# Layer 0's attention of a four-layer graph network: first masks on VectorE, cleared margins, a pool for early-freed tiles, 256-column matmuls

## The chip, the cores and the metric

The kernel runs on one core of one Trainium2 chip. A core has five engines with a queue each, worked off in order: TensorE (PE in the profile; PEld is its weight load), VectorE (DVE), ScalarE (ACT), GpSimd (POOL) and SyncE (SP, here only a queue of DMAs). They meet through semaphores. The metric is the device time of the kernel in microseconds, lower is better; the profiler's span of one execution stands beside it.

## What is computed

The reference has four layers over 16 graphs of 1024 nodes with 128 features. Each layer adds its result to x and normalises the rows.

```python
x = _layernorm(x + _L0_gnn_ref(x, adj, ...))              # attention over neighbours
x = _layernorm(x + _L1_gnn_ref(x, adj, nodemask, ...))    # dilated pattern, three convolutions
x = _layernorm(x + _L2_gnn_ref(x, adj, ...))
x = _layernorm(x + _L3_gnn_ref(x, adj, ...))

def _L0_gnn_ref(node_features, adjacency, ...):
    h_self = node_features @ W_self_w + W_self_b
    h_nb = node_features @ W_nb_w + W_nb_b
    pre = (h_self @ A1_i)[:, :, None, :] + (h_nb @ A1_j)[:, None, :, :] + A1_b
    scores = (relu(pre) @ A2_w)[..., 0] + A2_b[0]
    scores = where(adjacency == 0, -1e9, scores)
    attn = softmax(scores, axis=-1)
    return relu(h_self + einsum('bij,bjf->bif', attn, h_nb))
```

Only layer 0 is changed, and how layer 1's first stage gets its memory. The adjacency is sparse: an edge exists with a chance of about 0.8%, and it exists in both directions or in none, so the kernel handles edges and not pairs of nodes.

## The kernel before

Four phases follow each other: `phase_att` (layer 0), `phase_pattern` (the dilated pattern of layer 1), `phase_conv` (its convolutions) and `phase_end` (the rest of layer 1, and layers 2 and 3). A layer of tiles and pools records the operations, a scheduler orders each engine's instructions when the program is built, and waits are put in from what each tile's readers and writers are. Within an engine the built order is fixed.

**Blocks of attention.** The 1024 nodes of a graph are cut into NG = 10 groups of W = 104 (the last has 88). A block is a pair of groups (i, j) with i <= j; there are 55 for a graph, of which ten are diagonal (i = j, "one way": each edge is met once, in the direction in which it counts). Five bands r of 11 blocks each hold the groups r and 9 - r. A band has three chunks of 4, 4 and 3 blocks. A block has at most 128 edges, one for a partition.

**masks(b)** (L261) reads ten strips of the transposed adjacency into `ld` (two buffers), turns them into 0 and 1 in `mt` (L268), takes the diagonal out (L270), and writes the strip to `mask_d` in memory for the pattern phase (L271). All of it is on POOL and the SP queue. There are two mask tiles MT, cleared whole at the start (L162), and two tiles QS (L165).

**projections(b)** (L274): for ten groups, one fp32 matmul of the group's features with four weight matrices side by side (L287, 512 columns: h_nb, the two halves of `pre`, h_self), then one BF16 matmul of ones with the rows `bias3` (L288, 512 columns, of which the first and third quarter are zeros). ACT and DVE split the result into two fp32r parts (L291, L295).

**blocks(b, r)** (L306) finds the edges of a band: counts (L315, needs all ten masks), ranks (L345, written to `qs` by L348), slots (L327, L368), and the one-hot tiles of both ends of every edge (L376, L380).

**gather(b, r, lo, hi)** (L403) fetches, block by block, the projected rows of both ends of 128 edges: two matmuls with the one-hot tile of the own end (L423), two with that of the other end (L428), 384 columns each, into one PSUM bank `pg` of four quarters. Quarters 1 and 2 are then `pre` in the two directions, quarters 0 and 3 the neighbours' values. DVE makes the scores (L436), ACT the exponentials (L440) and the weighted values (L442). A diagonal block uses quarters 1 and 3 alone.

**scatter** (L447) sums the weighted values to the nodes (L455, fp32, two passes a matmul) into three PSUM banks; **collect** copies them out, **finish** (L477) does the softmax's division, the residual and the normalisation on POOL and DVE, and writes `x1_d` and, transposed, `x1T_d`.

The main loop weaves these generators: the gather of one chunk runs beside the scatter of the one before, the masks and projections of the next graph, the blocks of the next band, and the finish of the graph before. Ahead of it stand, for graph 0, masks and projections together, and then blocks(0, 0).

**Pools.** `phase_att` has one pool `cp` for what lives long and others that rotate. `phase_pattern` opens a pool `kp` for its constants and then `mp` with three buffers `m` of 16 KB a partition for whole masks (L743). They take the memory of the pools of attention, and a DMA into them waits for the last use of what lay there.

Of the kernel before, what the change touches and what calls it, by code (L numbers as in the profile page):

```python
# [10 lines left out]
F32 = mybir.dt.float32  # L11
F32R = mybir.dt.float32r
BF16 = mybir.dt.bfloat16
F16 = mybir.dt.float16
# [3 lines left out]
ALU = mybir.AluOpType  # L18
# [4 lines left out]
B, N, F = 16, 1024, 128  # L23
P = 128
# [68 lines left out]
NG, W, C = 10, 104, 128  # L93
# [4 lines left out]
UNITS = NG + 1  # L98
# [45 lines left out]
def phase_att(ctx, tc, t, c, x1_d, x1T_d, mask_d, flags):  # L144

    nc = tc.nc
    cp = ctx.enter_context(tc.tile_pool(name="t_c", bufs=1))
    lp = ctx.enter_context(tc.tile_pool(name="t_l", bufs=2))
    sm = ctx.enter_context(tc.tile_pool(name="t_s", bufs=4))
# [2 lines left out]
    ps_a = ctx.enter_context(tc.tile_pool(name="t_pa", bufs=1, space=PSUM))  # L152

    def load(name, shape, dtype=F16):
        w = cp.tile(shape, dtype, name=name)
        nc.sync.dma_start(w, t[name])
        return w


    MT = [cp.tile([P, NG, (NG - 1) * W + P], F16, name=f"mask{i}") for i in range(2)]  # L160
    for m in MT:
        nc.gpsimd.memset(m, 0.0)  # L162
    QS = [cp.tile([P, UNITS, C], F16, name=f"qs{i}") for i in range(2)]
    for q in QS:
        nc.gpsimd.memset(q, 0.0)  # L165
    k_rank = load("k_rank", [P, E])
    k_offs = load("k_offs", [P, P])
    k_step = load("k_step", [P, P])
    k_slot = load("k_slot", [P, C])
    k_slot_edge = load("k_slot_edge", [P, C], F32)  # L170
    k_id_col = load("k_id_col", [P, 1])
    w_all = cp.tile([P, 4 * F], F32, name="w_all")
    bias3 = cp.tile([P, 4 * F], BF16, name="bias3")
    off_diag = cp.tile([P, W], F16, name="off_diag")
    nc.vector.tensor_scalar(off_diag, c.ident[:, :W], 0.0, None, op0=ALU.is_equal)
    zeros = cp.tile([P, 512], BF16, name="zeros")
    nc.vector.memset(zeros, 0.0)
    ones = cp.tile([P, W], BF16, name="ones_w")
    nc.vector.memset(ones, 1.0)


# [1 line left out]
    k_id = load("k_id", [P, W])  # L183
    w_a2 = cp.tile([P, F], F32, name="w_a2")
    nc.sync.dma_start(w_a2, row_broadcast(t["L0_gnn_A2_w"], F))
    with tc.tile_pool(name="t_w", bufs=1) as wp:
        def weight(name, src, shape=[P, F]):
            w = wp.tile(shape, F32, name=name)
            nc.sync.dma_start(w, src)
            return w  # L190

        wsT = weight("wsT", t["wsT"])
        wnT = weight("wnT", t["wnT"])
        a1_i = weight("a1_i", t["L0_gnn_A1_w"][0:F, :])
        a1_j = weight("a1_j", t["L0_gnn_A1_w"][F : 2 * F, :])
        nc.sync.dma_start(w_all[:, :F], t["L0_gnn_W_nb_w"])
        nc.sync.dma_start(w_all[:, 3 * F :], t["L0_gnn_W_self_w"])
        pw = ps_w.tile([P, 512], F32, name="pw")
        nc.tensor.matmul(pw[:, :F], wsT, a1_i, start=True, stop=True)
        nc.tensor.matmul(pw[:, F : 2 * F], wnT, a1_j, start=True, stop=True)  # L200
        nc.scalar.copy(w_all[:, F : 3 * F], pw[:, : 2 * F])

        bs = weight("bs", t["L0_gnn_W_self_b"].rearrange("(p o) -> p o", o=1), [P, 1])
        bn = weight("bn", t["L0_gnn_W_nb_b"].rearrange("(p o) -> p o", o=1), [P, 1])
        bs_all = wp.tile([P, P], F32, name="bs_all", tag="wsT")
        nc.vector.tensor_copy(bs_all, bs.to_broadcast([P, P]))
        bn_all = wp.tile([P, P], F32, name="bn_all", tag="wnT")
        nc.vector.tensor_copy(bn_all, bn.to_broadcast([P, P]))
        a1_b = weight("a1_b", row_broadcast(t["L0_gnn_A1_b"], F))
        row_s = weight("row_s", row_broadcast(t["L0_gnn_W_self_b"], F))  # L210
        row_n = weight("row_n", row_broadcast(t["L0_gnn_W_nb_b"], F))
        pw = ps_w.tile([P, 512], F32, name="pw")
        nc.tensor.matmul(pw[:, :F], bs_all, a1_i, start=True, stop=False)
        nc.tensor.matmul(pw[:, :F], bn_all, a1_j, start=False, stop=True)
        bias = wp.tile([P, 2, F], F32, name="bias")
        nc.vector.tensor_tensor(bias[:, 0, :], pw[:, :F], a1_b, ALU.add)
        nc.vector.tensor_tensor(bias[:, 1, :], row_s, row_n, ALU.add)
        rows = wp.tile([P, 2, F], F32, name="rows")
        part = wp.tile([P, 2, F], BF16, name="part")
        for k in range(3):  # L220
            nc.vector.tensor_copy(part, bias)
            nc.vector.tensor_tensor(bias, bias, part, ALU.subtract)
            if k == 0:
                nc.vector.tensor_scalar(rows, part, c.ident[:, 0:1], None, op0=ALU.mult)
            else:
                nc.vector.scalar_tensor_tensor(
                    rows, part, c.ident[:, k : k + 1], rows, op0=ALU.mult, op1=ALU.add
                )
        nc.vector.memset(bias3, 0.0)
        nc.vector.tensor_copy(bias3.rearrange("p (a f) -> p a f", f=F)[:, 1:4:2, :], rows)  # L230

    self_edge = cp.tile([P, B, NG], F32, name="self_edge")
    nc.sync.dma_start(self_edge, t["adj_diag"])
# [27 lines left out]
    def masks(b):  # L261

        mt = MT[b % 2]
        for s in range(NG):
            n = W if s < NG - 1 else LAST
            ld = lp.tile([P, N], F32, name="ld")
            nc.sync.dma_start(ld[:n], t["adjT"][b, s * W : s * W + n, :])
            nc.gpsimd.tensor_scalar(mt[:n, s, :N], ld[:n], 0.0, None, op0=ALU.is_gt)  # L268
            d = mt[:n, s, s * W : (s + 1) * W]
            nc.gpsimd.tensor_tensor(d, d, off_diag[:n], ALU.mult)  # L270
            nc.sync.dma_start(mask_d[b, s * W : s * W + n, :], mt[:n, s, :N])  # L271
            yield

    def projections(b):  # L274

        d = S[b] = Consts()
        xT = lp.tile([P, NP], F32, name="xT", bufs=1)
        nc.sync.dma_start(xT, t["xTp"][b])
        d.parts = {}
        d.hs = lp.tile([P, NG, F], F32, name="hs")  # L280
        d.sc = lp.tile([P, BANDS * UNITS * 2], F32, name="sc")
        nc.vector.memset(d.sc, 0.0)
        d.off = lp.tile([P, BANDS * UNITS], F32, name="off")
        nc.vector.memset(d.off, 0.0)
        for s in (*range(4, NG), *range(4)):
            pw = ps_w.tile([P, 512], F32, name="pw")
            nc.tensor.matmul(pw[:W], xT[:, s * W : (s + 1) * W], w_all, start=True, stop=False)  # L287
            nc.tensor.matmul(pw[:W], ones, bias3, start=False, stop=True)  # L288
            hi = d.parts[s] = lp.tile([P, 2, 3 * F], F32R, name=f"parts{s}", bufs=1 if s < 4 else 2)
            z = sm.tile([P, F], F32, name="z_self", bufs=2)  # L290
            nc.scalar.copy(hi[:W, 0, :], pw[:W, : 3 * F])  # L291
            nc.scalar.copy(d.hs[:W, s, :], pw[:W, 3 * F :])
            nc.scalar.copy(z[:W], pw[:W, 2 * F : 3 * F])
            yield
            nc.vector.tensor_tensor(hi[:W, 1, :], pw[:W, : 3 * F], hi[:W, 0, :], ALU.subtract)  # L295

            nc.vector.tensor_tensor(z[:W], pw[:W, F : 2 * F], z[:W], ALU.add)
            k = b * NG + s
            nc.vector.scalar_tensor_tensor(
                z[:W], z[:W], 0.0, w_a2[:W], op0=ALU.max, op1=ALU.mult, accum_out=seen_self[:W, k : k + 1]  # L300
            )
            yield
# [89 lines left out]
        nc.scalar.copy(wide.ids, pw[:, : 2 * UNITS])  # L392
        yield

    def reversed_parts(x):

        return bass.AP(
            tensor=x.tensor, offset=x.offset + 2 * F, ap=[list(x.ap[0]), [-F, 3], [1, F]]
        )

    G = {}
# [1 line left out]
    def gather(b, r, lo, hi):  # L403

        d = S[b]
        wide = OH[b, r]
        todo = band(r)
        n = 2 * (hi - lo)
# [7 lines left out]
        for u in range(lo, hi):  # L416
            i, j = todo[u]
            own, other = wide.ends[:W, u, 0, :], wide.ends[:W, u, 1, :]

            pg = ps_g.tile([P, 4, F], F32, name="pg")  # L420
            flat = pg.rearrange("p a f -> p (a f)")
            for p in range(2):
                nc.tensor.matmul(  # L423
                    flat[:, : 3 * F], own, d.parts[i][:W, p, :], start=p == 0, stop=False,
                    skip_group_check=True,
                )
            for p in range(2):
                nc.tensor.matmul(  # L428
                    pg[:, 1:, :], other, reversed_parts(d.parts[j][:W, p, :]), start=False, stop=p == 1,
                    skip_group_check=True,  # L430
                )
            at = (r * UNITS + u) * 2
            ways = 2 if j > i else 1
            for e in range(ways):
                junk = sm.tile([P, F], F32, name="junk", bufs=2)
                nc.vector.scalar_tensor_tensor(  # L436
# [40 lines left out]
    def finish(b):  # L477
# [21 lines left out]
        for s0 in range(0, NG, 5):  # L499
            s = slice(s0, s0 + 5)  # L500
            shape = [W, 5, F]
            h = own[:W, s, :]
            nc.gpsimd.tensor_tensor(h, h, es[:W, s].unsqueeze(2).to_broadcast(shape), ALU.mult)
            nc.gpsimd.tensor_tensor(h, h, d.sums[:W, s, :F], ALU.add)
            yield
            nc.vector.tensor_tensor(h, h, rz[:W, s].unsqueeze(2).to_broadcast(shape), ALU.mult)
            yield
# [137 lines left out]
def phase_pattern(ctx, tc, t, c, mask_d, slots_d, x1_d, keep, flags):  # L645
# [3 lines left out]


    nc = tc.nc
    kp = ctx.enter_context(tc.tile_pool(name="q_k", bufs=1))
    mp = ctx.enter_context(tc.tile_pool(name="q_m", bufs=3))
    cp = ctx.enter_context(tc.tile_pool(name="q_c", bufs=1))
    wp = ctx.enter_context(tc.tile_pool(name="q_w", bufs=2))
    sm = ctx.enter_context(tc.tile_pool(name="q_s", bufs=4))
# [1546 lines left out]
```

## Time and profile before

| | |
|---|---|
| time, median of three | 3260.76 us (3250.69 to 3261.46) |
| span of the profiled execution | 3262.6 us, granted clock 0.921 |
| first gather matmul (L423) | 83.5 us |
| last scatter matmul ends (L455) | 1716.7 us |
| first matmul of the pattern phase (L749) | 1745.0 us |

How to read it: in the page's first section, busy time is given for each engine with its share of the span and the number of instructions. In the rows of groups stand line, engine, operation, out and in, shapes, count, busy time, mean duration in ns, and the idle time just before with what ended it. These are the rows of the lines concerned:

```profile
L268 POOL TENSOR_SCALAR mask<-ld 104x1024 f16<-104x1024 f32 (+1 forms) x160 | 464.9, 2906 | 331.6 <-PE pg L428 173.1
L423 PE MATMUL pg<-parts,oh 104*128 104x384 f32 x1760 | 560.2, 393 | 0.4 <-ACT hg L442 0.2
L428 PE MATMUL pg<-parts,oh 104*128 104x384 f32 x1760 | 498.6, 355 | 0.0
L288 PE MATMUL pw<-bias,ones_w 128*104 128x512 bf16 x160 | 63.4, 398 | 4.8 <-DVE bias L230 4.8
```

[...]the pace of PE is therefore read from starts. The granted clock is 1 at full speed and 0.5 at half.

### The profile page before, as it was taken

What the parts mean: (1) busy time and instruction counts of PE and PEld (TensorE: products, weight loads), DVE (VectorE), ACT (ScalarE), POOL (GpSimd) and SP (SyncE); (2) the same over time, 40 slices, a digit from 0 to 9 for tenths busy, and PEclk for the clock granted to TensorE, in tenths of its full rate; (3) what the DMA queues carried; (4) which work ended last, traced back from release to release, by engine and by line L of the source; (5) the groups of instructions that cost most, each with busy time, mean ns of one, the idle gap of its engine ahead of it and who ended that gap; (6) DMA issues with size and microseconds to landing.
All of it is one profiled execution on the core that took longest, in us unless ns stands there. A gap on an engine that the chain in (4) does not pass through costs nothing. (4 is left out here: it accounts for less than half of the span.)

```text
span 3262.6 us, 70599 instructions
## 1 busy us (share of the span) xinstructions
PE 2852.2 (87%) x25724; PEld 2516.6 (77%) x25724; DVE 2277.8 (70%) x8203; ACT 1785.6 (55%) x5608; POOL 1357.1 (42%) x1302
## 2 busy tenths in 40 slices
PE   3999999999999999999995859567877799999997
PEld 1878887778878887778885858356676799999997
DVE  3788788888878887888874476755655466666665
ACT  1777777777766776777771323135644343333332
POOL 7655554555545454554223332233432333322221
PEclk7999999999999999999996778788988899999999
DMA  4423332333222332322004433034443444444341
GB/s 122 121 81 84 99 89 55 84 87 105 81 60 77 97 97 60 84 81 73 21 21 166 163 105 117 27 119 149 161 158 117 156 170 170 153 168 163 141 157 37
DMA packets 162021, 348.60 MB, mean 107 GB/s; under 512 B 14708, under 2 KB 68230, under 8 KB 161536
## 3 DMA queue, kind: packets, MB, share of 16 engines
q1 hardware_dynamic: 150912, 315.57, 30.4%
q0 software_dynamic: 10752, 28.42, 3.0%
q8 instruction: 206, 3.38, 0.4%
q14 instruction: 151, 1.24, 0.1%
HBM read 257.87 MB, written 87.03 MB: 106 GB/s over the span
## 5 line engine op out<-in xcount | busy, mean ns | idle before, releaser
L268 POOL TENSOR_SCALAR mask<-ld 104x1024 f16<-104x1024 f32 (+1 forms) x160 | 464.9, 2906 | 331.6 <-PE pg L428 173.1
L423 PE MATMUL pg<-parts,oh 104*128 104x384 f32 x1760 | 560.2, 393 | 0.4 <-ACT hg L442 0.2
L455 PE MATMUL pa<-hg,we 128*104 128x129 f32 (+1 forms) x3520 | 551.4, 274 | 3.5 <-ACT hg L442 2.5
L436 DVE SCALAR_TENSOR_TENSOR junk<-pg,w_a 128x128 f32<-128x128 f32 x1600 | 402.7, 283 | 209.0 <-PE pg L428 206.3
L442 ACT ACTIVATE hg<-pg,hg 128x128 f32<-128x128 f32 x1600 | 511.7, 369 | 16.6
L455 PEld LDWEIGHTS pa<-hg,we 128*104 128x104 f32 x3520 | 494.8, 173 | 22.7 <-ACT hg L442 10.4
L428 PE MATMUL pg<-parts,oh 104*128 104x384 f32 x1760 | 498.6, 355 | 0.0
L428 PEld LDWEIGHTS pg<-parts,oh 104*128 104x128 f32 x1760 | 322.2, 192 | 1.4
L423 PEld LDWEIGHTS pg<-parts,oh 104*128 104x128 f32 x1760 | 286.8, 192 | 29.2 <-ACT hg L442 4.2
L440 ACT ACTIVATE hg<-sc 128x2 f32<-128x2 f32 (+1 forms) x880 | 186.5, 212 | 175.8 <-DVE junk L436 173.1
L410 DVE TENSOR_TENSOR we<-k_id,ids 128x832 f32<-128x832 f16 (+1 forms) x240 | 247.7, 1032 | 5.1 <-PE pa L455 3.5
L1332 POOL TENSOR_TENSOR rstd<-ve,mhalf 128x4 f32<-128x4 f32 x96 | 97.2, 1012 | 325.0 <-DVE ve L1331 324.9
L380 ACT CAST oh<-oh_b 104x1024 fp32r<-104x1024 bf16 (+1 forms) x240 | 223.2, 969 | 15.7 <-DVE oh_b L376 15.3
L287 PE MATMUL pw<-w_all,xT 128*104 128x512 f32 x320 | 178.5, 642 | 10.7 <-DMA xT<-in_xTp 8.2
L490 POOL TENSOR_TENSOR own<-parts 104x128 f32<-104x128 f32 x160 | 89.9, 597 | 222.5 <-DVE x_rows L510 211.0
L327 DVE TENSOR_TENSOR g<-k_slot,off 105x1408 f16<-105x1408 f16 x80 | 133.4, 1668 | 57.4 <-ACT off L323 57.4
L1336 DVE TENSOR_SCALAR x<-x,mv,rstd 128x128 f32<-128x128 f32 x256 | 104.7, 450 | 91.1 <-POOL rstd L1332 91.1
L376 DVE TENSOR_TENSOR oh_b<-pw,k_slot_edge 104x512 bf16<-104x512 f32 (+1 forms) x240 | 147.1, 635 | 10.1 <-PE pw L375 9.3
L355 DVE SCALAR_TENSOR_TENSOR one_way<-qs,mask 104x1040 bf16<-104x1040 f16 (+9 forms) x160 | 149.0, 931 | 1.0 <-ACT qs L348 0.9
L348 ACT CAST qs<-pw 104x416 f16<-104x416 f32 (+1 forms) x240 | 114.9, 479 | 63.1 <-PE pw L345 61.8
L369 ACT CAST oh_b<-pw 104x512 bf16<-104x512 f32 (+1 forms) x240 | 133.0, 555 | 18.3 <-PE pw L368 18.2
L1441 ACT ACTIVATE y<-x,shift,rstd 128x128 f32<-128x128 f32 x128 | 52.7, 482 | 163.4 <-POOL shift L1434 163.4
(352 smaller groups left out, 6777.9 us busy)
## 6 DMA issues: line engine op xcount, KB each, us to landing
ld<-in_adjT SPq DMA_DIRECT2D x144, 416.0 KB
m<-mask_d SPq DMA_DIRECT2D x16, 2048.0 KB
keep_adj<-in_adjT SPq DMA_DIRECT2D x8, 4096.0 KB
adj<-in_adjT SPq DMA_DIRECT2D x8, 4096.0 KB
mask_d<-mask SPq DMA_DIRECT2D x144, 208.0 KB
hT_d<-uT SPq DMA_DIRECT2D x48, 512.0 KB
h<-hT_d SPq DMA_DIRECT2D x48, 512.0 KB
hT<-hT_d SPq DMA_DIRECT2D x32, 512.0 KB
```

The source lines that it names most:

```text
L268: nc.gpsimd.tensor_scalar(mt[:n, s, :N], ld[:n], 0.0, None, op0=ALU.is_gt)
L287: nc.tensor.matmul(pw[:W], xT[:, s * W : (s + 1) * W], w_all, start=True, stop=False)
L355: nc.vector.scalar_tensor_tensor(junk[:W, :nb, :], q[:W, at : at + nb, :W], EDGE, mt[:W, i, i * W : NP].rearrange("p (n w) -> p n w", w=W) ...
L376: nc.vector.tensor_tensor(o[:W, n0 : n0 + m, 1, :], pw[:W, :m, :], k_slot_edge[:W].unsqueeze(1).to_broadcast([W, m, C]), ALU.is_equal,)
L380: nc.scalar.copy(wide.ends[:W, n0 : n0 + m], o[:W, n0 : n0 + m])
L410: nc.vector.tensor_tensor(we[:, :n, :], k_id.unsqueeze(1).to_broadcast([P, n, W]), wide.ids[:, 2 * lo : 2 * hi].unsqueeze(2).to_broadcast( ...
L423: nc.tensor.matmul(flat[:, : 3 * F], own, d.parts[i][:W, p, :], start=p == 0, stop=False, skip_group_check=True,)
L428: nc.tensor.matmul(pg[:, 1:, :], other, reversed_parts(d.parts[j][:W, p, :]), start=False, stop=p == 1, skip_group_check=True,)
L436: nc.vector.scalar_tensor_tensor(junk, pg[:, 1 + e, :], 0.0, w_a2, op0=ALU.max, op1=ALU.mult, accum_out=d.sc[:, at + e : at + e + 1],)
L440: nc.scalar.activation(hg[:, u - lo, :ways, F], d.sc[:, at : at + ways], AF.Exp)
L442: nc.scalar.activation(hg[:, u - lo, e, :F], pg[:, 3 - 3 * e, :], AF.Copy, scale=hg[:, u - lo, e, F : F + 1])
L455: nc.tensor.matmul(PA[bank][:W, at : at + part.stop - part.start], we[:, 2 * (u - lo) + e, :], hg[:, u - lo, e, part], start=False, stop=T ...
```

## The change

Six edits, all in attention or at its borders:

- **First masks on DVE.** For graph 0 the strips are loaded through ScalarE's queue and turned into masks by DVE; for the other graphs nothing changes. The purpose is that nothing at the start stands behind POOL.
- **Margins only.** Of MT and QS, only what no mask or rank ever writes is cleared.
- **A pool for early-freed tiles.** What is last used before attention's final steps lies in a pool `ep` opened first; `phase_pattern` opens `mp` ahead of `kp`, so that the mask buffers lie where `ep` was and can be filled before attention has ended.
- **Bias with 256 columns.** `bias3` holds the two quarters that aren't zero, and L288 adds into these two alone.
- **One-way blocks with 256 columns.** For a diagonal block, L423 computes quarters 1 and 2, and L428 adds to quarters 1 and 3.
- **The last finish on DVE.** For graph 15, two operations of `finish` go from POOL to DVE.

```diff
+    ep = ctx.enter_context(tc.tile_pool(name="t_e", bufs=1))
     cp = ctx.enter_context(tc.tile_pool(name="t_c", bufs=1))
...
-        w = cp.tile(shape, dtype, name=name)
+        w = (cp if name == "k_id" else ep).tile(shape, dtype, name=name)
...
-    MT = [cp.tile([P, NG, (NG - 1) * W + P], F16, name=f"mask{i}") for i in range(2)]
+    MT = [ep.tile([P, NG, (NG - 1) * W + P], F16, name=f"mask{i}") for i in range(2)]
     for m in MT:
-        nc.gpsimd.memset(m, 0.0)
-    QS = [cp.tile([P, UNITS, C], F16, name=f"qs{i}") for i in range(2)]
+        nc.gpsimd.memset(m[:W, :, N:], 0.0)
+        nc.gpsimd.memset(m[64:W, NG - 1, :N], 0.0)
+    QS = [ep.tile([P, UNITS, C], F16, name=f"qs{i}") for i in range(2)]
     for q in QS:
-        nc.gpsimd.memset(q, 0.0)
+        nc.gpsimd.memset(q[:W, :, W:], 0.0)
...
-    w_all = cp.tile([P, 4 * F], F32, name="w_all")
-    bias3 = cp.tile([P, 4 * F], BF16, name="bias3")
-    off_diag = cp.tile([P, W], F16, name="off_diag")
+    w_all = ep.tile([P, 4 * F], F32, name="w_all")
+    bias3 = ep.tile([P, 2, F], BF16, name="bias3")
+    off_diag = ep.tile([P, W], F16, name="off_diag")
...
-        nc.vector.memset(bias3, 0.0)
-        nc.vector.tensor_copy(bias3.rearrange("p (a f) -> p a f", f=F)[:, 1:4:2, :], rows)
+        nc.vector.tensor_copy(bias3, rows)
...
+        engine, queue = (nc.gpsimd, nc.sync) if b else (nc.vector, nc.scalar)
...
-            nc.sync.dma_start(ld[:n], t["adjT"][b, s * W : s * W + n, :])
-            nc.gpsimd.tensor_scalar(mt[:n, s, :N], ld[:n], 0.0, None, op0=ALU.is_gt)
+            queue.dma_start(ld[:n], t["adjT"][b, s * W : s * W + n, :])
+            engine.tensor_scalar(mt[:n, s, :N], ld[:n], 0.0, None, op0=ALU.is_gt)
...
-            nc.gpsimd.tensor_tensor(d, d, off_diag[:n], ALU.mult)
+            engine.tensor_tensor(d, d, off_diag[:n], ALU.mult)
...
-            nc.tensor.matmul(pw[:W], ones, bias3, start=False, stop=True)
+            nc.tensor.matmul(
+                pw[:W].rearrange("p (a f) -> p a f", f=F)[:, 1::2, :], ones, bias3, start=False, stop=True,
+                skip_group_check=True,
+            )
...
-            tensor=x.tensor, offset=x.offset + 2 * F, ap=[list(x.ap[0]), [-F, 3], [1, F]]
+            tensor=x.tensor, offset=x.offset + 2 * F, ap=[list(x.ap[0]), [-F * step, 4 - step], [1, F]]
...
+            ways = 2 if j > i else 1
+            first, step = (0, 1) if ways == 2 else (F, 2)
             for p in range(2):
                 nc.tensor.matmul(
-                    flat[:, : 3 * F], own, d.parts[i][:W, p, :], start=p == 0, stop=False,
+                    flat[:, first : 3 * F], own, d.parts[i][:W, p, first:], start=p == 0, stop=False,
...
-                    pg[:, 1:, :], other, reversed_parts(d.parts[j][:W, p, :]), start=False, stop=p == 1,
+                    pg[:, 1::step, :], other, reversed_parts(d.parts[j][:W, p, :], step), start=False,
...
-            nc.gpsimd.tensor_tensor(h, h, es[:W, s].unsqueeze(2).to_broadcast(shape), ALU.mult)
-            nc.gpsimd.tensor_tensor(h, h, d.sums[:W, s, :F], ALU.add)
+            engine = nc.gpsimd if b < B - 1 else nc.vector
+            engine.tensor_tensor(h, h, es[:W, s].unsqueeze(2).to_broadcast(shape), ALU.mult)
+            engine.tensor_tensor(h, h, d.sums[:W, s, :F], ALU.add)
...
+    mp = ctx.enter_context(tc.tile_pool(name="q_m", bufs=3))
     kp = ctx.enter_context(tc.tile_pool(name="q_k", bufs=1))
-    mp = ctx.enter_context(tc.tile_pool(name="q_m", bufs=3))
```

More of the change, by code (lines that the diff above doesn't have):

```diff
@@ L171, in phase_att @@
     k_id_col = load("k_id_col", [P, 1])
-    w_all = cp.tile([P, 4 * F], F32, name="w_all")
-    bias3 = cp.tile([P, 4 * F], BF16, name="bias3")
-    off_diag = cp.tile([P, W], F16, name="off_diag")
+    w_all = ep.tile([P, 4 * F], F32, name="w_all")
+    bias3 = ep.tile([P, 2, F], BF16, name="bias3")
+    off_diag = ep.tile([P, W], F16, name="off_diag")
     nc.vector.tensor_scalar(off_diag, c.ident[:, :W], 0.0, None, op0=ALU.is_equal)
-    zeros = cp.tile([P, 512], BF16, name="zeros")
+    zeros = ep.tile([P, 512], BF16, name="zeros")
     nc.vector.memset(zeros, 0.0)
-    ones = cp.tile([P, W], BF16, name="ones_w")
+    ones = ep.tile([P, W], BF16, name="ones_w")
     nc.vector.memset(ones, 1.0)
@@ L286, in projections @@
             pw = ps_w.tile([P, 512], F32, name="pw")
-            nc.tensor.matmul(pw[:W], xT[:, s * W : (s + 1) * W], w_all, start=True, stop=False)
-            nc.tensor.matmul(pw[:W], ones, bias3, start=False, stop=True)
+            nc.tensor.matmul(
+                pw[:W], xT[:, s * W : (s + 1) * W], w_all, start=True, stop=False, skip_group_check=True
+            )
+            nc.tensor.matmul(
+                pw[:W].rearrange("p (a f) -> p a f", f=F)[:, 1::2, :], ones, bias3, start=False, stop=True,
+                skip_group_check=True,
+            )
             hi = d.parts[s] = lp.tile([P, 2, 3 * F], F32R, name=f"parts{s}", bufs=1 if s < 4 else 2)
@@ L393, in blocks, with reversed_parts @@
         yield
-    def reversed_parts(x):
+    def reversed_parts(x, step=1):
         return bass.AP(
-            tensor=x.tensor, offset=x.offset + 2 * F, ap=[list(x.ap[0]), [-F, 3], [1, F]]
+            tensor=x.tensor, offset=x.offset + 2 * F, ap=[list(x.ap[0]), [-F * step, 4 - step], [1, F]]
         )
@@ L428, in gather @@
                 nc.tensor.matmul(
-                    pg[:, 1:, :], other, reversed_parts(d.parts[j][:W, p, :]), start=False, stop=p == 1,
-                    skip_group_check=True,
+                    pg[:, 1::step, :], other, reversed_parts(d.parts[j][:W, p, :], step), start=False,
+                    stop=p == 1, skip_group_check=True,
                 )
             at = (r * UNITS + u) * 2
-            ways = 2 if j > i else 1
             for e in range(ways):
```

## The prediction

> **What bounds the kernel now.** I read the busy shares first, then busy time by stretch, then the timelines of the three places that the change touches. One core runs, so no core or die has to be told apart.
>
> ```profile
> PE 2852.2 (87%) x25724; PEld 2516.6 (77%) x25724; DVE 2277.8 (70%) x8203; ACT 1785.6 (55%) x5608; POOL 1357.1 (42%) x1302
> 0.00:83.50 83.50, 28.93 (x98) 12.28 (x98) 31.81 (x77) 14.36 (x43) 66.10 (x50) 0.72 0.46 124
> 83.50:1716.70 1633.20, 1563.09 (x12591) 1321.66 (x12588) 1331.32 (x5325) 1204.65 (x4018) 811.42 (x627) 0.97 0.28 77
> 1716.70:1745.00 28.30, 2.74 (x10) 1.81 (x10) 13.09 (x41) 2.42 (x8) 8.47 (x9) 0.54 0.47 165
> 1745.00:3262.00 1517.00, 1257.45 (x13028) 1180.88 (x13028) 901.59 (x2760) 564.19 (x1542) 471.10 (x617) 0.88 0.39 137
> ```
>
> The columns of the stretches are length, then busy PE, PEld, DVE, ACT, POOL, then granted clock, DMA share, GB/s. Four stages follow each other. Until 83.5 us POOL is the busy engine. From the first gather matmul (83.5) to the last scatter matmul (1716.7) PE is busy 96%, DVE 82%, ACT 74%: PE sets the pace, 1633.2 / 16 = 102.1 us a batch. For 28.3 us nearly nothing runs. The remaining 1517 us (pattern, convolution, end) are not edited, so I only shift them.
>
> The start, in the PE timeline and the POOL timeline:
>
> ```profile
> 0.97 8.96 POOL L162 MEMSET mask<- 128x10640 f16 x1
> 10.23 9.02 POOL L162 MEMSET mask<- 128x10640 f16 x1
> 72.96 2.76 POOL L268 TENSOR_SCALAR mask<-ld 88x1024 f16<-88x1024 f32 x1 [1.52 <-DMA ld<-in_adjT]
> 75.78 0.19 PE L315 MATMUL pw<-k_rank,mask 104*128 104x1 f16 x1 [4.57 <-POOL mask L268]
> ```
>
> PE waits for POOL's last mask of batch 0. Two whole-tile clears (18 us) come before the first mask, then each of ten masks costs 2.8 us. The projections had ended at 44.4.
>
> The steady stage, PE's timeline inside one band:
>
> ```profile
> 1656.52 0.52 PE L428 MATMUL pg<-parts,oh 104*128 104x384 f32 x2
> 1656.88 0.61 PE L455 MATMUL pa<-hg,we 128*104 128x129 f32 x4
> 1657.24 0.59 PE L423 MATMUL pg<-parts,oh 104*128 104x384 f32 x2
> ```
>
> Read starts, not durations, which overlap: two 384-column matmuls take 0.36 us from start to start, about 0.176 each (median of the trace); the 129-column fp32 passes 0.11; a 512-column BF16 one (L288) 0.216.
>
> The end of attention:
>
> ```profile
> 1731.18 2.74 PE L536 MATMUL pw<-ident,x_rows 104*128 104x104 f32 x10 [14.52 <-DVE x_rows L523]
> 1731.18 10.45 SPq L743 DMA_DIRECT2D m<-mask_d  x3
> 1745.05 1.85 PE L749 MATMUL pu<-q_run,m 128*128 128x1 f16 x64 [11.13 <-issue]
> ```
>
> The pattern phase's first loads leave at 1731.2, after attention's last pool has been freed; its first matmul runs 13.9 us later.
>
> [...]LDWEIGHTS:[...] The trace shows records of 189 ns at 128 columns and 170 at 104[...].
> - [...]DVE's L221 cast takes 4.08 us beside POOL's clear, 0.86 to 1.0 after it.
>
> **The change part by part.**
>
> *Start (clears, first masks on DVE and ScalarE's queue).* POOL's 18 us of clears shrink to the margins (2 x 1,424 columns instead of 2 x 10,640, some 2.5 us). Ten masks leave POOL for DVE. No DVE row has this shape; the nearest are L508 (640 columns 0.81 us, so 1.3 at 1024)[...]; I take 1.1. Added: 20 DVE instructions, about 13 us, in a stretch where DVE is busy 31.8 of 83.5. Loads now bind: an ld takes about 4.2 us from issue to use (53.42 to 57.67), two buffers, so a buffer turns over in 4.2 + 1.1 + 0.5 = 5.8 us and ten masks need about 5 + 4 x 5.8 + 2, some 30 us, up to 36 where DVE stands in order behind the bias chain and ScalarE holds an ld behind a projection's copies. Queued behind a waiting mask on DVE are the second halves of projections, for which PE waits; behind a waiting ld on ScalarE are their first halves. The bias rows, without POOL beside them, are ready near 25 instead of 27.7. The projections then take the 16.7 us they take now (27.7 to 44.4), so they end near 42, and with the waits 43; the first blocks take 7.3 (76.2 to 83.5). Gather starts near 50: **34 us** earlier (26 if masks run late, 42 if the clock stays up).
>
> *Bias, 512 to 256 columns.* 160 instructions, 10 of them in the start: 150 x (216 - 109) = 16 us of PE.
>
> *One-way blocks, 384 to 256 columns.* Ten diagonal blocks a batch, four matmuls each: 640. Unknown: the interval at 256 columns. Floor 110[...], ceiling 160 (the 189 ns record mostly binds). In proportion it is 117[...]; I take 120: 640 x 56 = 36 us. Ends: 10 and 42.
>
> Together 52 us on the engine that sets the pace. DVE and ACT do the same work and get 3% less room (DVE 82 to 85%), so I count 0.9: **47 us**.
>
> *Order at a batch's start.* The built program moves instructions. The waits of PE between 160 and 1600 us name one stall of up to 3.1 us a batch, 14 in all:
>
> ```profile
> PE pw L375 <- DVE oh_b L376: 42.1, 14, 3.1
> ```
>
> DVE is late there since L506, ahead of L376 in its queue, waits for POOL's sum. In the new order L376 stands ahead of L508 (0.81 us) in 13 batches: 13 x 0.8 = 10, of which I take **8**. The stall's main part stays.
>
> *Pools.* Tiles last used early lie together, and the three m buffers (48 KB a partition) fit into their 53 KB. In the built program the first m load waits for L386 of the last band (1700.1 now) instead of the final reduction of seen_z (1727.9 to 1728.2). Three loads of 2 MB at the 276 GB/s of 1740 to 1760 need 23 us and are in by about 1725. What then holds the first L749 is q_run, still issued after the seen_z reduction, and the third x1T copy, which waits for a buffer whose store now lands at 1740.6 because it shares the DMA engines with m; alone it needs 2 to 3 us. So L749 starts near 1736: **9 us** (5 to 16).
>
> *Last finish on DVE.* POOL's 2.8 us add leaves the chain, two DVE adds of 0.8 enter, and the small DVE operations beside it stop being slowed (L493 1.46 us there against 0.16 in mid-stage): under 1 us, counted in the 9.
>
> Sum: 34 + 47 + 8 + 9 = 98 us. 3260.8 - 98 = **3163 us**.
>
> **The rivals.**
> - *Weight loads set the pace.* For it: PEld is busy 81% of the stage and its record is longer than the matmul interval. Against it: 129-column passes run at 110 ns with records of 170. One-way saving near 0: 34 + 14 + 8 + 9 = 65, 3196 us.
> - *The start is bound by loads.* For it: only two ld buffers, ScalarE in order. Against it: masks need only be done by 43. Gain 20 instead of 34: 3177 us.
> - *All comes true and more.* PE stays warm from the projections into the gather (granted clock 0.50 from 47 to 94 now), the full 52 count, and m loads help more: 42 + 52 + 10 + 16 = 120, 3141 us.
> - *Slower.* The stage runs at a granted clock of 0.97. Each drop now follows the 3 us stall. A new order that lets PE idle oftener could take it to 0.88: 1580 x (0.97 / 0.88 - 1) = 162 us lost against 98 gained, 3325 us. Nothing in the built order points to new stalls of that length.
>
> **How the numbers follow.** Forecast 0.62, weights 0.14, loads 0.12, more 0.09, slower 0.03. The range 3138 to 3200 holds all but the slower case and tails, with a few us for the spread of the runs (3250.7 to 3261.5). Faster by over 0.5%: 0.95; within it 0.02; slower 0.03.
>
> **What would show it.** First gather matmul near 50 us, waiting no more on POOL's masks. The 256-column one-way matmuls 115 to 125 ns from start to start, the bias 109. Attention from first gather to last scatter near 1578 us. First L749 about 19 us after the last scatter. The later stages unchanged in length. Wrong, if the stage's DVE share rises past 90% with PE idle, or if the one-way interval stays above 160.

## The result, and the profile after

The changed kernel takes 3208.8 us (median of four, 3201.6 to 3217.2), the kernel before 3255.7 in the same series: a ratio of 0.986 (95% interval 0.982 to 0.990), 47 us gained where 98 were forecast. The sign was right, the size a little under half, and 3208.8 lies above the range. The times here and below are medians of four executions or more; one execution of e2 took 8998 us and is left out of its ratio.

The stretches of the changed kernel, with the columns of before (length, then busy PE, PEld, DVE, ACT, POOL, granted clock, DMA share, GB/s):

```profile
0.00:57.60 57.60, 25.88 (x98) 11.08 (x98) 30.87 (x96) 14.17 (x43) 20.36 (x31) 0.90 0.70 191
57.60:1678.60 1621.00, 1523.70 (x12592) 1300.19 (x12588) 1313.55 (x5327) 1198.69 (x4018) 775.53 (x626) 0.96 0.29 81
1678.60:1696.80 18.20, 2.74 (x10) 1.82 (x11) 11.96 (x43) 2.37 (x7) 5.12 (x6) 0.57 0.35 116
1696.80:3199.00 1502.20, 1248.62 (x13028) 1174.27 (x13028) 895.40 (x2760) 563.68 (x1542) 470.80 (x618) 0.89 0.39 136
```

| stretch | before | after | change | forecast |
|---|---|---|---|---|
| start to first gather matmul | 83.5 | 57.6 | -25.9 | -34 |
| attention, first gather to last scatter | 1633.2 | 1621.0 | -12.2 | -55 |
| last scatter to first L749 (now L760) | 28.4 | 18.2 | -10.2 | -9 |
| the rest, not edited | 1517.5 | 1502.9 | -14.6 | 0 |

The last row is spread, not gain: in the profiles of the eleven kernels below, none of which edits these stages, they take 1497 to 1524 us. Without it the profile gives 48 us, close to the 47 of the times. So the loss is in attention: 43 of its 55 us did not come, though PE's busy time there fell by 39 us. Its idle time rose by 27, from 70.1 to 97.3.

From here on a stop is an idle time of PE of more than 0.9 us, and half clock is time at which the record of the granted clock says 0.5. Line numbers have moved with the edit: of the lines named below, L376, L490, L508, L510, L520 and L523 of the kernel before are L385, L500, L519, L521, L531 and L534 of the changed one.

What PE waited for, between 160 and 1600 us of the changed kernel (us in total, times, longest):

```profile
PE pg L434 <- ACT hg L452: 48.8, 14, 3.6
PE pw L384 <- DVE oh_b L385: 37.7, 27, 2.6
```

The second line is the known stop at a batch's start (L384 was L375), now 2.55 us instead of 3.11. The first line is new: once a batch the gather stops for 3.5 us. It names ACT, but ACT is only the last link. DVE's waits point to the cause, first in the kernel before, then in the changed one:

```profile
DVE x_rows L523 <- POOL rstd L520: 23.5, 14, 1.7
```

```profile
DVE x_rows L534 <- POOL rstd L531: 74.2, 14, 5.4
```

One such place in the timelines of the changed kernel (start, duration, and in brackets the idle time before and what ended it), PE, DVE and POOL one after the other:

```profile
507.17 0.42 PE L439 MATMUL pg<-parts,oh 104*128 104x384 f32 x1
511.07 1.01 PE L434 MATMUL pg<-parts,oh 104*128 104x384 f32 x2 [3.48 <-ACT hg L452]
```

```profile
484.21 0.79 DVE L519 TENSOR_TENSOR own<-own,hs 104x640 f32<-104x640 f32 x1
...
495.90 1.29 DVE L385 TENSOR_TENSOR oh_b<-pw,k_slot_edge 104x512 bf16<-104x512 f32 x2
497.11 0.81 DVE L521 SCALAR_TENSOR_TENSOR x_rows<-own,x_rows 104x640 f32<-104x640 f32 x1
...
503.48 0.08 DVE L446 DVE_READ_ACCUMULATOR junk<-pg,w_a 128x1 f32 x1
508.84 0.86 DVE L534 TENSOR_SCALAR x_rows<-x_rows,mv,rstd 104x128 f32<-104x128 f32 x3 [5.29 <-POOL rstd L531]
```

```profile
498.00 6.09 POOL L500 TENSOR_TENSOR own<-parts 104x128 f32<-104x128 f32 x10 [2.64 <-DVE x_rows L521]
504.04 2.47 POOL L514 TENSOR_TENSOR own<-own,es 104x640 f32<-104x640 f32 x2
506.48 0.25 POOL L529 TENSOR_SCALAR ve<-mv 104x10 f32<-104x10 f32 x1
506.82 1.99 POOL L531 TENSOR_TENSOR rstd<-ve,mhalf 104x10 f32<-104x10 f32 x1
```

And POOL at the same point of a batch in the kernel before:

```profile
517.07 5.67 POOL L490 TENSOR_TENSOR own<-parts 104x128 f32<-104x128 f32 x10 [13.82 <-DVE x_rows L510]
522.70 4.03 POOL L503 TENSOR_TENSOR own<-own,es 104x640 f32<-104x640 f32 x2
...
529.79 0.39 POOL L270 TENSOR_TENSOR mask<-mask,off_diag 104x104 f16<-104x104 f16 x1
535.48 0.25 POOL L518 TENSOR_SCALAR ve<-mv 104x10 f32<-104x10 f32 x1 [5.31 <-DVE mv L79]
```

Read it backwards from PE. The gather has three pg buffers; a pg is freed when ACT has made its hg, which needs DVE's L446 for the score. DVE works in order and stands at L534 for rstd, so no L446 runs for 5.3 us, and PE runs out of pg. POOL is late because L500 and L514, which prepare the *next* graph's finish in the one `own` buffer, stand ahead of this graph's L529. They start when DVE's second L521 frees `own`. In the kernel before, that instruction (L510) followed its L508 within 1 us, POOL was done with everything by 530.2 and idled 5.3 us until mv came. In the new order L521 comes 13 us after L519, behind two L385 of the next band, and POOL is still busy when mv is ready.

The half clock follows. In the trace's record of the granted clock, attention spends 131.7 us at 0.5 in 30 stretches (before: 89.1 in 15), two in a batch instead of one.

### The profile page after: what moved, and what is told of

Read it like the earlier page. It is cut to its first block, busy times and chain, and to the rows that moved or that the text cites. A ratio compares the mean times of both kernels' runs of the same rounds, so it can differ in the third digit from the quotient of the medians.

```text
span 3199.7 us, 70693 instructions
## 1 busy us (share of the span) xinstructions
PE 2800.9 (88%) x25724; PEld 2487.4 (78%) x25724; DVE 2251.8 (70%) x8226; ACT 1778.9 (56%) x5608; POOL 1271.8 (40%) x1280
## 5 line engine op out<-in xcount | busy, mean ns | idle before, releaser
L272 POOL TENSOR_SCALAR mask<-ld 104x1024 f16<-104x1024 f32 (+1 forms) x150 | 443.2, 2955 | 548.1 <-PE pw L354 236.1
L434 PE MATMUL pg<-parts,oh 104*128 104x384 f32 (+1 forms) x1760 | 539.0, 382 | 49.7 <-ACT hg L452 49.1
L465 PE MATMUL pa<-hg,we 128*104 128x129 f32 (+1 forms) x3520 | 569.4, 277 | 1.8
L446 DVE SCALAR_TENSOR_TENSOR junk<-pg,w_a 128x128 f32<-128x128 f32 x1600 | 405.2, 283 | 173.3 <-PE pg L439 170.1
L452 ACT ACTIVATE hg<-pg,hg 128x128 f32<-128x128 f32 x1600 | 509.8, 370 | 17.1
L439 PE MATMUL pg<-parts,oh 104*128 104x384 f32 (+1 forms) x1760 | 473.2, 343 | 0.0
L434 PEld LDWEIGHTS pg<-parts,oh 104*128 104x128 f32 x1760 | 282.2, 193 | 78.4 <-ACT hg L452 62.0
L439 PEld LDWEIGHTS pg<-parts,oh 104*128 104x128 f32 x1760 | 314.6, 193 | 0.0
L419 DVE TENSOR_TENSOR we<-k_id,ids 128x832 f32<-128x832 f16 (+1 forms) x240 | 228.5, 952 | 8.5 <-PE pa L465 4.7
L291 PE MATMUL pw<-w_all,xT 128*104 128x512 f32 x320 | 185.6, 664 | 17.0 <-DMA xT<-in_xTp 8.3
L385 DVE TENSOR_TENSOR oh_b<-pw,k_slot_edge 104x512 bf16<-104x512 f32 (+1 forms) x240 | 144.6, 635 | 9.6 <-PE pw L384 7.1
L500 POOL TENSOR_TENSOR own<-parts 104x128 f32<-104x128 f32 x160 | 96.9, 637 | 118.4 <-DVE x_rows L521 82.4
L378 ACT CAST oh_b<-pw 104x512 bf16<-104x512 f32 (+1 forms) x240 | 133.1, 556 | 13.6 <-PE pw L377 13.5
```

The lines of the kernel that those rows point to most:

```text
L272: engine.tensor_scalar(mt[:n, s, :N], ld[:n], 0.0, None, op0=ALU.is_gt)
L419: nc.vector.tensor_tensor(we[:, :n, :], k_id.unsqueeze(1).to_broadcast([P, n, W]), wide.ids[:, 2 * lo : 2 * hi].unsqueeze(2).to_broadcast( ...
L434: nc.tensor.matmul(flat[:, first : 3 * F], own, d.parts[i][:W, p, first:], start=p == 0, stop=False, skip_group_check=True,)
L439: nc.tensor.matmul(pg[:, 1::step, :], other, reversed_parts(d.parts[j][:W, p, :], step), start=False, stop=p == 1, skip_group_check=True,)
L446: nc.vector.scalar_tensor_tensor(junk, pg[:, 1 + e, :], 0.0, w_a2, op0=ALU.max, op1=ALU.mult, accum_out=d.sc[:, at + e : at + e + 1],)
L452: nc.scalar.activation(hg[:, u - lo, e, :F], pg[:, 3 - 3 * e, :], AF.Copy, scale=hg[:, u - lo, e, F : F + 1])
```

## The experiments

For each kernel: its time, the ratio to the kernel before as timed in the same series (3248.6 to 3259.0 us) with its interval, and from its profile the length of attention, PE's stops in 14 batches (sum), and the time at half clock in attention. Each kernel has one profile. Where attention has the same work, its length differs by 2 to 6 us from profile to profile (changed and e6, before and e2), so smaller differences say nothing.

| kernel | time | ratio | attention | stops | half clock |
|---|---|---|---|---|---|
| before | 3255.7 | 1 | 1633.2 | 42 | 89 |
| changed | 3208.8 | 0.986 (0.982-0.990) | 1621.0 | 83 | 132 |
| e1 columns alone | 3262.3 | 1.0007 (0.9995-1.0018) | 1629.9 | 83 | 148 |
| e2 columns undone | 3224.3 | 0.989 (0.986-0.993) | 1627.6 | 42 | 76 |
| e3 rstd first | 3171.8 | 0.976 (0.970-0.983) | 1577.4 | 49 | 59 |
| e4 e3 + sums on DVE | 3154.8 | 0.967 (0.964-0.970) | 1564.0 | 17 | 58 |
| e5 e4 + own*es on DVE | 3111.4 | 0.957 (0.954-0.960) | 1522.9 | 0 | 9 |
| e6 first loads on SyncE | 3209.5 | 0.988 (0.985-0.991) | 1619.2 | 83 | 130 |
| e7 before, rstd three times | 3340.5 | 1.027 (1.024-1.030) | 1716.8 | 107 | 162 |
| e8 e5 + e6 | 3104.5 | 0.956 (0.953-0.959) | 1519.9 | 0 | 13 |
| e9 e5, first loads on GpSimd | 3099.5 | 0.952 (0.948-0.956) | 1520.9 | 0 | 15 |
| e10 e5, columns undone | 3134.7 | 0.963 (0.959-0.967) | 1543.4 | 0 | 9 |
| e11 e5, one-way blocks undone | 3132.6 | 0.962 (0.958-0.966) | 1543.0 | 0 | 11 |

**e1, the column edits alone, on the kernel before.**

```diff
+                pw[:W].rearrange("p (a f) -> p a f", f=F)[:, 1::2, :], ones, bias3, start=False, stop=True,
...
+            first, step = (0, 1) if ways == 2 else (F, 2)
...
+                    flat[:, first : 3 * F], own, d.parts[i][:W, p, first:], start=p == 0, stop=False,
```

> The kernel before with the 256-column edits alone (bias and one-way blocks); start, pools and last finish as before. In its built order the second half of L510 stands after two of the three L376 of the next band, as in the changed kernel, so the edit alone turns the order. Theory A (the saving is turned into a new wait by the order): attention from first gather to last scatter about 1620 us (1610 to 1630) instead of 1633; PE has two gaps over 2 us in a batch, the second of 3 to 4 us behind DVE's wait for POOL's rstd; half clock in attention about 130 us; total 12 to 18 us below before. Rival B (the start, pool or finish edits disturb attention, the columns deliver): attention 1580 to 1590 us, one gap in a batch, half clock near 80 us; total 45 to 55 us below before. Rival C (256 columns bring nothing on PE): the gap doesn't appear and attention stays at 1633.

Both stops are there, to the hundredth those of the changed kernel; PE's busy time in attention is 33 us shorter, attention 3 us, and the times can't tell the two kernels apart. The waits of PE in e1:

```profile
PE pg L429 <- ACT hg L447: 48.9, 14, 3.6
PE pw L379 <- DVE oh_b L380: 37.6, 27, 2.6
```

DVE waits 74.2 us for rstd (L525), the same figure as in the changed kernel. So the column edits turn the order by themselves: L515, which is L510 of the kernel before, now stands behind two L380 of the next band. Rival B falls. Theory A's 12 to 18 us did not come either; half clock is 148 us, not 130.

**e2, the changed kernel without the column edits** (`first, step = 0, 1` and a `bias3` of 512 columns).

> The changed kernel with the column edits undone (bias of 512 columns, one-way blocks of 384); start, pools and last finish stay. Its built order in the steady stage is that of before. Theory A: attention about 1633 us with one gap of 3.5 us in a batch and half clock near 80 us; the start stays near 57.6 us and the first pattern matmul 18 us after the last scatter; total only some 10 to 15 us above the changed kernel. Rival B: attention rises by about 50 us above the changed kernel's 1621 or stays with two gaps in a batch.

As theory A has it: one stop of 3.1 us in a batch, rstd waited for as before (23.5 us), start 59.6, 18.0 from the last scatter to the pattern phase's first matmul. So of the changed kernel's 47 us the other edits carry some 35. What is left for the columns as built, some 12, is not clear of the spread (the intervals of the two ratios overlap), and e1 shows none.

**e3, rstd ahead of the next sums.** One order edge (a rule that one instruction is issued after another) on POOL, nothing else edited:

```diff
-            nc.gpsimd.tensor_tensor(own[:W, s, :], d.parts[s][:W, 0, :F], d.parts[s][:W, 1, :F], ALU.add)
+            with (tc.issue_after(RSTD[0].ins) if RSTD else nullcontext()):
+                nc.gpsimd.tensor_tensor(own[:W, s, :], d.parts[s][:W, 0, :F], d.parts[s][:W, 1, :F], ALU.add)
```

Here `RSTD` holds the instruction that made the last rstd.

> The changed kernel with one order edge more on POOL: the sums own (L500) of a finish are issued after rstd (L531) of the finish before. DVE's and PE's built order is the same as in the changed kernel. Theory A: DVE's wait of 5.3 us for rstd falls under 1.5 us, PE's second gap (3.9 us in a batch) goes, and with it the half-clock stretch behind it; half clock in attention about 80 us instead of 132; attention 1621 - 15 x 3.9 - 26 = about 1537 us (1535 to 1560); total 60 to 85 us below the changed kernel. Rival C (the columns bring nothing, another engine carries the batch of 103 us): attention within 10 us of 1621, the gap moves elsewhere. Rival D (half clock comes from how much PE works, not from its stops): gap gone, half clock still about 130 us, attention 1560 to 1580.

DVE waits 27.6 us for rstd in 15 waits, not 74.2 in 14. The gather's stop is gone, and 44 us of attention with it. PE's waits of e3:

```profile
PE pw L384 <- DVE oh_b L385: 39.3, 28, 2.6
PE pw L550 <- DVE x_rows L537: 14.7, 15, 1.0
PE pw L291 <- ACT x1T L552: 11.9, 14, 1.1
```

Half clock fell further than expected (59, with 80 expected), so rival D falls, though attention lies in the band that D named. It is 1577, not 1537: of the 49 us of stop some 30 came back as shorter waits for DVE and ACT at the transposes (L550) and the projection behind them.

**e4, the addition of the sums on DVE for all graphs.**

```diff
-            engine.tensor_tensor(h, h, d.sums[:W, s, :F], ALU.add)
+            nc.vector.tensor_tensor(h, h, d.sums[:W, s, :F], ALU.add)
```

> As e3, and the addition of the sums (L515) on DVE for all graphs instead of POOL, so that DVE's L517 at a batch's start no longer waits for POOL behind a mask. Theory A: PE has no gap over 1.5 us in a batch, half clock in attention below 40 us, attention another 30 to 60 us below e3. Rival E (DVE is the next bound: two more additions of 0.8 us a batch in its queue): the gap at the batch's start stays or moves, attention within 15 us of e3.

The stop at the batch's start is gone, but attention gained 13 us, not 30 to 60, and half clock stayed at 58 us: rival E's "the gap moves" came true. It moved to the transposes, where POOL's own*es (L517, 890.88 to 893.35 in this batch) runs beside DVE. DVE and PE of e4:

```profile
891.21 1.01 DVE L537 TENSOR_SCALAR x_rows<-x_rows,mv,rstd 104x128 f32<-104x128 f32 x1
892.14 1.36 DVE L308 SCALAR_TENSOR_TENSOR z_self<-z_self,w_a 104x128 f32<-104x128 f32 x1
```

```profile
893.82 0.44 PE L550 MATMUL pw<-ident,x_rows 104*128 104x104 f32 x1 [1.24 <-DVE x_rows L537]
```

L308 takes 0.29 us at the median of its 160 in the changed kernel. Here it takes 1.36: it starts at 892.14, while POOL's two L517 run, and ends at 893.50, 0.15 us after them. That POOL's L517 holds up the DVE operations beside it is the author's reading; e5 takes L517 off POOL.

**e5, own*es on DVE as well** (`engine = nc.vector`).

> As e4, and the products own*es (L514) on DVE for all graphs as well. In e4 they run on POOL beside DVE's L537 (1.01 us) and L308 (1.36 us, otherwise 0.28), and PE's one remaining stop over 1 us, 1.24 us once a batch before the transposes L550, waits for these. Theory A (that stop and its half clock come from POOL and DVE running side by side there): the stop falls under 0.5 us, half clock in attention from 58 to 10 to 30 us, attention from 1564 to about 1525 to 1545. Rival E (DVE is the bound: two more products of 0.8 us a batch): the time moves to another wait for DVE, attention 1555 or more.

Theory A, a little beyond its range (1525 to 1545 us of attention, 10 to 30 us of half clock). No stop is left, and one stretch of half clock remains after the start. The stretch of attention in e5:

```profile
58.70:1581.60 1522.90, 1479.16 (x12591) 1263.19 (x12588) 1337.29 (x5386) 1196.42 (x4018) 701.21 (x564) 1.00 0.30 86
```

**e7, the suspected cost added to the kernel before.**

```diff
+        for _ in range(3):
+            nc.gpsimd.tensor_tensor(rstd[:W], ve[:W], c.mhalf[:W, 0:1].to_broadcast([W, NG]), ALU.pow)
```

> The kernel before, with rstd (L520) computed three times in a row on POOL, the last result kept: some 5.6 us more ahead of DVE's L523, once a batch, nothing else changed; the built order is that of before. DVE waits some 2 us for rstd in each batch now. Theory A (a DVE that waits 5 us and more for rstd stops PE once more in a batch): a second PE stop of 3.5 to 6 us in a batch at about +45 us, half clock in attention 130 to 170 us instead of 89, attention 70 to 120 us longer than 1633, total 3330 to 3380. Rival H (the second stop of the changed kernel is a matter of the new PE order or of the columns, DVE's wait is absorbed by its slack of 18%): attention within 15 us of 1633.

The order is that of before and the columns are 384 and 512; only rstd comes later. DVE waits up to 5.7 us, PE stops once more in a batch, and attention grows by 83.6 us:

```profile
PE pw L339 <- ACT qs L348: 60.5, 13, 4.7
```

Rival H falls. The new stop is not in the gather, as in the changed kernel, but in blocks (L339); DVE's wait for rstd is what the two have in common. The run also gives an estimate of what half clock costs: PE does the same work, its busy time in attention is 1586.2 instead of 1563.1, and half clock is 162.0 instead of 89.1, so a microsecond at half clock cost 23.1 / 72.9 = 0.32 us.

**e10 and e11, what the columns are worth without stops.**

> As e5, with the column edits undone (bias of 512 columns, one-way blocks of 384). Theory A (the columns save what was counted, 52 us of PE, wherever PE isn't stopped by an engine that is waited for): attention 45 to 60 us longer than e5's 1523, about 1568 to 1583, no stop over 1.5 us; total near 3160. Rival C (without stops another engine would carry the pace and the columns save little): under 20 us longer.

> As e5, with the one-way blocks alone back at 384 columns, the bias at 256. Theory A: 640 matmuls x 56 ns = 36 us of PE more; attention 30 to 42 us longer than e5's 1523, total near 3147, and the rest to e10 (16 us) is the bias.

Both missed: attention is 20.5 and 20.1 us longer than in e5, not 45 to 60 and 30 to 42. Rival C's "under 20" came nearest. The stretch of attention in e10, to be read against e5's:

```profile
58.60:1602.10 1543.50, 1517.22 (x12592) 1292.84 (x12588) 1324.30 (x5386) 1205.47 (x4018) 692.70 (x564) 1.00 0.30 84
```

PE's busy time is 34.9 us shorter in e5 than in e11 (1514.1): the one-way saving is the 36 counted. But PE's idle time is 43.7 in e5 and 28.9 in e11. With PE faster, short waits take 15 us back, most of them for ACT: it ended 38.5 us of e5's idle time and 26.0 of e11's, DVE 5.1 and 2.5 (ACT is busy 79% and DVE 88% of e5's stage). The bias is worth 3 us of busy time between e10 and e11, and 0.4 of length, though its interval fell from 216 to 109 ns. The built orders of these two differ: in e11 PE waits 17.1 us for ACT at L377, in e10 0.2 at the same line (L378 there), while the scatter's wait for ACT falls from 15.9 to 2.4. What hides the bias stays open.

**e6, e8 and e9, the start.** In e6 the first masks' loads go back to SyncE's queue (`engine, queue = nc.gpsimd if b else nc.vector, nc.sync`); e8 is e5 with this; in e9, e5 with the loads on GpSimd's queue, ahead of the first sums there.

> The changed kernel with the first masks' loads on SyncE's queue as in the kernel before; DVE still makes the masks. In the changed kernel ten loads of 416 KB stand on ScalarE's queue from 0.7 us on, SyncE's small loads are issued later than before (row_n at 15.7 us instead of 9.2, xT at 17.4 instead of 10.7), and row_n lands 8 us after its issue. Theory F (the 8 us that the start fell short come from these loads running ahead of the small ones): row_n is issued near 9.3, xT near 10.7, the first bias matmul starts at 21 to 25 us instead of 28.8, first gather 49 to 53 us instead of 57.6; total 4 to 9 us below the changed kernel. Rival G (the masks set the start, ten in a row behind two buffers): the last mask is ready later, first gather 56 us or later.

PE of the changed kernel and of e6 at the start:

```profile
28.83 0.37 PE L294 MATMUL pw<-bias,ones_w 128*104 128x256 bf16 x1 [1.24 <-DVE bias L232]
...
36.98 2.00 PE L291 MATMUL pw<-w_all,xT 128*104 128x512 f32 x2 [3.93 <-DVE z_self L306]
```

```profile
21.37 0.42 PE L294 MATMUL pw<-bias,ones_w 128*104 128x256 bf16 x1
...
46.95 0.18 PE L324 MATMUL pw<-k_rank,mask 104*128 104x1 f16 x1 [5.53 <-DVE mask L272]
```

Theory F is right on the loads: row_n is issued at 9.2 us again, and the bias is there 7.5 us earlier. Rival G is right on the start: now the masks are last, and the gather starts at 55.7, not at 49 to 53. The total doesn't move.

> e5 and e6 together (rstd ahead of the next sums, both products and sums on DVE, first loads on SyncE's queue). If the gains add: e5's time less 4 to 9 us, about 3105 to 3130. If rival G holds or e5 gives nothing: 3150 or more.

3104.5, just under the expected range, but its interval overlaps e5's, so a gain over e5 isn't shown; the profiles have 2 us in the start and 3 in attention.

> As e5 (rstd ahead of the next sums, own*es and the addition of the sums on DVE), with the first masks' ten loads on GpSimd's queue, ahead of the first sums there. SyncE then has only small loads and stores ahead of xT, and the masks' loads do not stand behind stores as in e6. Theory F+G (the start is set by both the late small loads and the rate of mask loads, so that both have to go): row_n issued near 9.3 us, first bias matmul at 21 to 25, last mask near 36 to 42, first gather 46 to 52 us; total 6 to 12 us below e5. If DMA bandwidth alone sets the start (about 4.2 MB of masks and 2.1 MB stored): first gather 55 or later, total as e5.

Missed: 55.3, with row_n issued at 11.7 and not 9.3. The first bias matmul is at 21.8, but the third mask load leaves only at 19.2, when the first mask frees its buffer, because DVE's order has the first mask inside the bias chain:

```profile
4.81 1.43 POOL L271 DMA_DIRECT2D ld<-in_adjT  x2
19.19 0.55 POOL L271 DMA_DIRECT2D ld<-in_adjT  x1 [12.95 <-DVE part L224]
```

So each load from the third on waits for one of the two buffers, as the prediction's rival on loads had it; a kernel with more buffers wasn't run, and bandwidth as the limit, the expectation's other case, isn't excluded. e9 has the lowest time here, but 12.8 of its 18 us of span below e5 lie in stages that neither edits, so it is e5's equal, with a start some 3 us shorter.

## Why the prediction was right or wrong

- **Start, 34 forecast, 26 measured.** The mechanism held, and a mask takes DVE 0.69 us, not the 1.1 that the prediction took. Mis-sized: the bias, taken as ready near 25 and first used at 28.8 (the small loads leave later, row_n at 15.7 instead of 9.2), and the projections, 21.0 us instead of 16.7, with the wait of 3.9 us behind a mask load on DVE that the prediction named and priced at 1. The first blocks took 7.8 (7.3 forecast).
- **Column intervals: right.** 256-column one-way matmuls start 119 to 120 ns apart, bias ones 109 (120 and 109 were taken, the author's estimates); 384-column ones stay at 176.
- **Columns, 52 counted as 47: the step that failed.** The count of PE's work was right: from before to e1 PE's busy time falls by 32.9 us while half clock grows by 58.6, which at e7's price is 51.7 us less work; from e2 to the changed kernel the same sum gives 53.6. What failed is the factor 0.9, by which nearly all of that work was to become time: it supposed that PE goes on setting the pace and that DVE and ACT only have 3% less room. In the kernel as built, e1 shows a gain near 0, since PE now stops once more in a batch, 48.9 us in all, for a DVE that waits for rstd. With every stop removed e10 shows 20.5, a factor of 0.4; but there DVE has more work than in the kernel before, so this factor is e5's, not the kernel's before.
- **Order at a batch's start, 8: right, and not enough.** The stop fell from 42.1 to 34.2 us in 14 batches. But the prediction followed one moved instruction, L376 ahead of L508, and not the other, the second L510 behind two L376. That one delays `own`, then rstd, then DVE, then PE; e3 and e7 show it, the first by taking the delay out, the second by putting it in.
- **The slower rival's last sentence was false.** "Nothing in the built order points to new stalls of that length": the built order had one of 3.5 us a batch, and the rival's mechanism, half clock behind it, came with it. At e7's price the added 43 us of half clock cost some 14, an estimate. The terms of attention then make 52 + 8 - 49 - 14 = -3 against 12 measured. Of the 15 us between, 11 are shorter waits: PE's idle time outside the stops fell from 23.8 to 12.6 us. That the other engines catch up during the stops would explain it and isn't shown.
- **e3's attention, 1577.4, is the forecast's 1578: in part luck.** Once the missed stop is gone, the forecast length comes out. But e3's half clock is 30 us shorter than before, some 30 us of other waits came, the forecast counted neither, and e3 with the old columns wasn't run.
- **Pools, 9 forecast, 10 measured; last finish and later stages: right.** The first m load leaves at 1662.6, ahead of the last scatter's end, and L760 starts 18.2 us after that end (19 forecast), held at the end by the x1T copy, not by m. The store that this copy waits for took 2.3 us from issue (1693.85) to release (1696.17); in the kernel before, with the m loads in flight and a DMA share of 0.88, it took 7.3 (1733.22 to 1740.56).

## What to carry to other kernels

In a kernel whose order is planned when it is built, an edit that only shortens matmuls can re-plan the other engines, as e1 shows: compare the order of every engine that feeds the bound one, and follow each moved instruction through the buffer it frees to the next waiter, above all where an in-order engine waits for a slower helper. Take a small result that another engine waits for (rstd) ahead of bulk work (the next sums) by an explicit order edge. A saving on an engine that is 96 to 98% busy need not become time: here, with no stop left, 0.4 of it did, since other engines at 79 and 88% were not always ready.

## What the runs showed of the hardware

- Half clock comes in steps. In each profile all stretches of half clock begin on a common grid of 3.41 us and last a multiple of it, but for the last, which ends with the profile.
- Short stops are followed by half clock. Stops of 2.55 us came with half clock in 13 of 13 batches of the changed kernel and in 8 of 13 of e3, and e4's stop of 1.24 us, with 0.9 to 1.2 us of shorter gaps in the ten us before, in 9 of 14.
- The idle share of one window of that grid tells the cases apart. In the attention stages of all thirteen profiles, without their first and last 8 us, PE was idle for at least half of 141 windows at full clock, and half clock followed all 141; for 40 to 50% of 28 windows, and it followed 16; for less than 40% of 5580 windows, and it followed 5. A stop of 1.62 us in the kernel before (at 1540.19) lay across a line of the grid, with 36 and 12% of idle in the two windows, and no half clock followed; one of 1.62 us in the changed kernel (at 1603.64) lay in one window, with 48%, and half clock followed. Whether e3's five stops of 2.55 us without half clock lay across a line isn't shown. Of windows at half clock with under 10% idle, 159 of 183 were followed by full clock, of those with over 20% none of 36. (Idle as the profile has it, whose ends of matmuls are modelled.)
- DVE makes a mask (88 to 104 x 1024, fp32 to fp16) in 0.69 to 0.75 us, POOL in 2.77 at the median and 3.96 at most in the changed kernel.
